# A four-layer graph network on one core: the second power of the adjacency by seven block products, and a last pair stored in two halves

## The chip, the core and the metric

The kernel runs on one core of a Trainium2 chip. A core has a matrix engine (TensorE, here PE, with a separate row PEld for its weight loads), three engines for elementwise work (VectorE or DVE, ScalarE or ACT, GpSimd or POOL) and an engine SyncE (SP) that here issues every DMA. Each engine executes its own queue in order; engines wait for each other through semaphores. The metric is the device time of one execution in microseconds (us). Times of the kernel before: 1476.92, 1478.15 and 1479.26 us, median 1478.15.

## The reference

The input is `x` of 64 graphs x 256 nodes x 128 features, with one 256 x 256 adjacency matrix `adj` (A below) for all of them. There are four layers, and each ends in a layer norm of `x + layer(x)`. All is in float32.

- Layer 0: five steps of a gated recurrent unit, each with a product of A and the state, then products with 128 x 128 weights, two sigmoids and a tanh.
- Layer 1: attention whose 256 x 256 matrix is made from A alone; products with it and with two weights.
- Layer 2: a graph attention with a softmax over 256 nodes per graph, then an isomorphism layer with another product with A, two weights and norms.
- Layer 3: a Chebyshev-like polynomial, in which both adjacencies are A:

```
parts = [x, A x, A^2 x, A^3 x, A x, A^2 x, A^3 x]
y     = sum_k parts[k] @ weight[:, :, k]
x     = layernorm(x + y)
```

The kernel forms q = A x and uses the second power of A: `x + y` is `x V0 + q V1 + A^2 (x V2 + q V3)`, with weights that are added up beforehand (the identity goes into V0). The last product, with A^2, is what the first part of the change is about.

## The kernel before

The 64 graphs are worked on in 32 pairs. One pair's features fill a tile of 128 partitions x 512 float32: two graphs, two blocks of 128 nodes each, 128 features. No loop over pairs orders the work. Instead the program records every operation of every pair as an `Op` in a `Schedule` (`S.add`, L120), with the values that it reads and writes, one or more ways to execute it (an engine, a planned cost in us and the function that issues it), and then a planner (`Schedule.order`, L161) simulates the engines with the planned costs and writes out one fixed order for each engine. At each step it takes the operation that can start first, and among equals the one whose due time `late` is earliest. Due times are set by pair (`due`, L139): 15 us apart, and `LAST_DUE` apart for the last twelve pairs. In every window of 15 us of the plan an entry of the table `SEEDS` (L63) can shift the due times by a fixed pseudo-random amount; another table of seeds gives another order. Operations with several ways, for example the sums that can go to DVE or POOL, go to the engine that the planner expects to finish first. `DVE+` marks a DVE operation for which the planner also books a port shared with POOL.

Intermediate values live in shared tiles (38 of the class A of 512 columns, eight PSUM banks of 512 columns, and others) that the planner assigns. Layouts are turned between token-major and feature-major in most places by DVE's 32 x 32 transpose and two DMA passes through DRAM (`turn`, L554 to L580).

Products of a pair with a 256 x 256 matrix are done in one of two ways:

- `spread` (L582) takes four matmuls of 256 columns (L588): for each graph, two blocks of the sum.
- `spread7` (L593) takes seven matmuls of 128 columns (L606), by Winograd's form of Strassen's scheme for 2 x 2 blocks. Sums of blocks of the right matrix are made once (`winograd`, L500). Per use it needs three sums of blocks of the state ahead of the products (L612 to L614), and copies and sums behind them (L620 to L627). Sums of SBUF operands alone are offered to DVE or POOL; copies out of PSUM (`evacuate`, L268) to ACT or DVE.

The table `SEVEN` (L24) says for how many of the last pairs the plain form is kept, by place.

Layer 3 (`layer3`, L888) turns x, forms q with `spread7`, and for pairs 0 to 29 calls `polynomial7` (L919). That computes the two products of [x q] with the weights again in seven block products (`product`, L937, whose matmuls are at L940), into the PSUM bank `y` (the part without A^2) and the tile `rr` (the part to be multiplied by A^2, written by DVE at L957 and L959). Then four matmuls of 256 columns (L963) add A^2 `rr` onto `y` in PSUM; `scale_norm` (L712) norms `y` and `store` (L884) writes the pair's 256 KB. A norm here needs no mean, since the weights are centred: it takes squares with an accumulated sum on ACT (L685), or statistics on DVE (L679); an added epsilon and a power of -0.5 on POOL (L690, L693); and a scaling on ACT (L705) or DVE (L707). The last two pairs, 30 and 31, go through the plain form in `layer3` (matmuls at L903, L904 and L911) with the same norm over the whole pair and one store.

Of the kernel before, what the change touches and what calls it, by code (L numbers as in the profile page):

```python
# [8 lines left out]
AF = mybir.ActivationFunctionType  # L9
# [11 lines left out]


FAST = (0, 1, 2, 3, 4)
SEVEN = {"q1": 4, "g": 4, "q3": 4, "pr": 2}  # L24
FIRST, FINAL = 1, 0
L1 = -1

# [22 lines left out]
SPARE = {"DVE": 1.0, "DVE+": 0.0, "POOL": -0.3}  # L50


DUE, LAST_DUE, LAST = 15.0, 12.0, 12

MARGIN, LAG = 1.1, 0.3

HOLD = (0.0, -20.0, 0.0, 40.0)

WINDOW, NUDGE = 15.0, 1.0

XLOAD, TLOAD = (0.6, 1.33, 2.5), (0.6, 1.05, 1.5)

SEEDS = [0, 113, 0, 0, 0, 0, 0, 0, 0, 0, 0, 0, 0, 0, 0, 0, 0, 0, 0, 0, 0, 0, 0, 0, 0, 0, 0, 0, 99747, 109039, 0,  # L63
         127395, 136626, 145860, 0, 172027, 0, 0, 192033, 202672, 213506, 0, 0, 0, 0, 0, 0, 0, 0, 0, 0, 0, 0, 0,
         0, 0, 0, 0, 0, 0, 0, 0, 0, 0, 431775, 441535, 451905, 0, 0, 0, 0, 0, 0, 516963, 526274, 0, 544854, 0, 0,
         0, 585026, 0, 0, 0, 622370, 631520, 639000, 646717, 658660, 667211, 0, 681297, 690347, 700377, 708021,
         726295, 727034, 736340, 0]


def mm(cols, n=1):  # L70
# [42 lines left out]
class Schedule:  # L113
# [47 lines left out]
    def order(self, tiles):  # L161

        self.prepare()
        engines = dict.fromkeys([*SEEN, "PORT"], 0.0)
        free = {cls: [(0.0, k) for k in range(len(ts))] for cls, ts in tiles.items()}
        ready, full, moved, out, window = [op for op in self.ops if not op.before], set(), 0.0, [], 0

        def slots(v):
            return [s for s in free[v.cls] if not v.seeded or (v.cls, s[1]) in full]

        while ready:
            best, homes, seed = None, {}, SEEDS[window] if window < len(SEEDS) else 0
            for op in ready:
                held = op.since
                for v in op.holds:
                    if v.home is None:
                        if (v.cls, v.seeded) not in homes:
                            homes[v.cls, v.seeded] = min((s for s, _ in slots(v)), default=1e9)
                        held = max(held, homes[v.cls, v.seeded])
                if held == 1e9 or best and held > best[0][0]:  # L180
                    continue
                way = None
                for engine, us, uses, spare, fn in op.plans:
                    start = max(held, *(engines[e] for e in uses))
                    if way is None or start + us + spare < way[0]:
                        way = start + us + spare, start, engine, us, uses, fn
                late = op.late
                if seed and op.pair >= 0:
                    late += NUDGE * (1 + seed % 3) * shuffled(op.number, seed)
                key = (way[1], late, op.number)  # L190
                if best is None or key < best[0]:
                    best = key, op, way
            if best is None:
                raise RuntimeError("the shared tiles are too few for this order")
            (start, _, _), op, (_, _, engine, us, uses, fn) = best
            if start >= (window + 1) * WINDOW:
                window += 1
                continue
            ready.remove(op)
            for v in op.holds:  # L200
                if v.home is None:
                    slot = min(slots(v), key=lambda s: s[0])
                    free[v.cls].remove(slot)
                    v.home, v.ap = slot[1], tiles[v.cls][slot[1]]
            end, base = start + us, engine.rstrip("+-")
            for e in uses:
                engines[e] = end
            seen = SEEN[base] + LAG
            if op.dma:
                wait, move, after = op.dma  # L210
                moved = max(moved, end + wait) + move * MARGIN
                seen = moved + after - end + LAG
            out.append((start, op.number, op, fn))
            for v in op.holds:
                v.left, v.end = v.left - 1, max(v.end, end + seen)
                if not v.left:
                    free[v.cls].append((v.end, v.home))
                    (full.add if v.full or v.seeded else full.discard)((v.cls, v.home))
            for x in op.then:
                same = engine != "SP" and x.base == base  # L220
                x.waits, x.since = x.waits - 1, max(x.since, end + (AGAIN.get(base, 0.0) if same else seen))
                if not x.waits:
                    ready.append(x)
        self.span = max(engines.values())
        return [(op, fn) for _, _, op, fn in sorted(out, key=lambda x: x[:2])]
# [11 lines left out]
def kernel(ctx: ExitStack, tc: tile.TileContext, x, xT, adj, adjT, mats, cols, rows, out):  # L237
# [54 lines left out]
        return rbc.ap[:, None, i * D:(i + 1) * D].to_broadcast([P, n, D])  # L292

    def load(o, i, v, kb=256, dma=None):
        S.add([("SP", 0.45, lambda: nc.sync.dma_start(o(), i))], [], [v], dma or (0.6, kb / 245, 0.9))

    xs = [Value("X", name=f"x{p}") for p in range(n_pairs)]
    hTs = [Value("T", name=f"hT{p}") for p in range(n_pairs)]
# [201 lines left out]
    def winograd(v, name):  # L500
# [5 lines left out]
                                                                             op0=ALU.mult, op1=ALU.subtract), [v, o], [o])  # L506
        dve(0.25, lambda: nc.vector.tensor_add(o.ap[:, 3, :], o.ap[:, 1, :], blk(1, 0)), [v, o], [o])
        return o
    aT7, offT7, ginT7 = winograd(aT, "aT7"), winograd(offT, "offT7"), winograd(ginT, "ginT7")
    centre(vx, lambda: vx.ap, 2)  # L510
    centre(vq, lambda: vq.ap, 2)
    vt = fixed([4, D], "vt")
# [30 lines left out]
    def tokens(v):  # L543
        return v.at(4, D)
# [9 lines left out]
    def turn(i, name, site, n=512):  # L554


        o = Value("A", name=name) if n == 512 else i
        if not by_dma(site):
            ts = [Value("PS", name="ps") for _ in range(n // 512)]
            for k, t in enumerate(ts):  # L560
                def fn(k=k, t=t):
                    for c in range(4):
                        nc.tensor.transpose(tokens(t)[:, c, :], i.at(n // P, P)[:, 4 * k + c, :], ident.ap)  # L563
                pe(TURN, fn, [i, ident], [t])
            for k, t in enumerate(ts):
                evacuate(lambda k=k: o.at(n)[:, 512 * k:512 * k + 512], lambda t=t: t.at(512), [t], [o])
            return o
        st, d = Value("A" if n == 512 else "B", name="turn"), Value("E", name="turn")
        dve(n / 512 * 0.55 + 0.09, lambda: nc.vector.transpose(st.at(n), i.at(n)), [i], [st])  # L569
        blocks = lambda *ap: bass.AP(tensor=d.ap.tensor, offset=d.ap.offset, ap=ap)  # L570
        S.add([("SP", 0.4, lambda: nc.sync.dma_start(blocks([P, P], [P * P, n // P], [1, P]), st.at(n // P, P)))],
              [st], [d], (0.6, n / 512 * 0.86, 0.5))

        def move():
            for q in range(4):
                b = blocks([P, 32], [32 * P, n // 32], [1, 32])
                nc.sync.dma_start(o.at(n // 32, 32)[32 * q:32 * q + 32],  # L577
                                  bass.AP(tensor=b.tensor, offset=b.offset + 32 * q, ap=b.ap))
        S.add([("SP", 2.1, move)], [d], [o], (-0.8, n / 512 * 1.5, 0.9))
        return o  # L580

    def spread(i, right):  # L582
# [229 lines left out]
    def layer2(x2):  # L812
# [14 lines left out]
        u, s = Value("B", name="u"), Value("S", name="nm")  # L827
        line = lambda *ap: bass.AP(tensor=d.ap.tensor, offset=d.ap.offset, ap=ap)
        dve(0.25, lambda: nc.vector.transpose(srow.at(4, 32), hs()[:, :, D - 30:D + 2]), [h], [srow])
        S.add([("SP", 0.45, lambda: nc.sync.dma_start(line([32, 4], [P, 4], [1, 32]), srow.at(4, 32)[31::32]))], [srow], [d], (0.5, 0.1, 0.5))  # L830
        S.add([("SP", 0.45, lambda: nc.sync.dma_start(sd.at(512), line([0, P], [1, 512])))], [d], [sd], (0.9, 0.7, 1.2))

        nm, den = (lambda k=k: s.at(32)[:, 4 * k:4 * k + 4] for k in range(2))
        d2v = Value("S", name="d2")
# [47 lines left out]
        layer_norm(y, x2)  # L882

    def store(o, p):  # L884
        S.add([("SP", 0.4, lambda: nc.sync.dma_start(out[2 * p:2 * p + 2].rearrange("b (t p) d -> p (b t) d", p=P), tokens(o)))],
              [o], [], (0.6, 1.0, 0.9))

    def layer3(x3, p):  # L888
# [19 lines left out]
        for i, t in enumerate(ts):  # L908
            def fn(i=i, t=t):
                for j in range(2):  # L910
                    nc.tensor.matmul(t.at(512)[:, :N], a2T.ap[:, j, i * P:(i + 1) * P], rr.at(2, N)[:, j],  # L911
                                     start=False, stop=(j == 1), skip_group_check=True)
            pe(mm(256, 2), fn, [a2T, rr, t], [t])
        s, rs = scale_stats([(t, range(i, 4, 2)) for i, t in enumerate(ts)])
        for i, t in enumerate(ts):
            scale_tokens(t, o, range(i, 4, 2), s, rs)
        store(o, p)

    def polynomial7(xT, qT, p):  # L919

# [36 lines left out]
        dve(0.335, lambda: nc.vector.tensor_add(R(1), blocks(t, 0), blocks(sv, 0)), [t, sv], [rr])  # L957
        product(t, 0, S4, VQ(1), [s4])
        dve(0.335, lambda: nc.vector.tensor_add(R(0), blocks(t, 0), blocks(sv, 1)), [t, sv], [rr])  # L959
        for i in range(2):  # L960
            def fn(i=i):
                for j in range(2):
                    nc.tensor.matmul(y.at(2, 2, D)[:, :, i, :], a2T.ap[:, j, i * P:(i + 1) * P], rr.at(2, 2, D)[:, j],  # L963
                                     start=False, stop=(j == 1), skip_group_check=True)
            pe(mm(256, 2), fn, [a2T, rr, y], [y])
        scale_norm(y, o)
        store(o, p)

    for p in range(n_pairs):
        S.pair = p  # L970
# [54 lines left out]
```

## Time and profile before

| | |
|---|---|
| median of three runs | 1478.15 us |
| the profiled execution | 1477.2 us |
| its span, first to last instruction | 1475.4 us |
| mean granted TensorE clock | 0.999 |
| PE busy | 1463.8 us, 99% |
| DVE busy | 1265.9 us, 86% |
| ACT busy | 1052.5 us, 71% |
| POOL busy | 931.5 us, 63% |
| mean DMA rate | 147 GB/s |
| L963, matmuls with A^2 | 240 instructions of 128x256, 59.6 us busy |
| L606, matmuls of `spread7` | 3346 instructions of 128x128, 275 ns each |
| L270, copy of 128x512 from PSUM on ACT | 592 ns |
| L621, sum of 128x256 | 464 ns on DVE, 751 ns on POOL |
| L625, sum of 128x128 | 321 ns on DVE, 512 ns on POOL |
| L693, power of 128x4 on POOL | 1073 ns |

The profile lists one execution, taken by the hardware profiler. Times are counted from the first instruction of the span. A line such as `L606 PE` names the line of the kernel that issued the instruction and the engine. The busy time of PE is a union over instructions that overlap; the pace at which matmuls follow each other is read from the chain of work, where each piece has the time that it adds. The chain follows the last instruction back to what released it, step by step. In the list of waits, "A <- B" means that A could have started but for B. A row by stretch gives the length, and then busy time and the number of instructions of each engine.

### The profile page before, as it was taken

The page shows a single profiled execution, that of the slowest core. Times are in us where ns is not written, and L with a number is a line of the kernel's source. Part 1 is how long each engine was busy: PE and PEld are TensorE (multiplying, and loading weights), DVE is VectorE, ACT ScalarE, POOL GpSimd, SP SyncE. Part 2 cuts the span into 40 slices and gives each one's busy share as a digit, 9 for nine tenths or more (in the row PEclk, how much of TensorE's full clock was granted, in tenths as well). Part 3 has the DMA queues.
Part 4 walks back from the last instruction along what each step waited for, and adds up shares of the span by engine and source line. Part 5 has one row for each costly group of instructions (what it writes and reads, how often), then busy time and mean ns, then how long its engine had stood idle before and what let it go on. Part 6 is the DMA issues. An engine that isn't in the chain of part 4 may idle for free.

```text
span 1475.4 us, 28934 instructions
## 1 busy us (share of the span) xinstructions
PE 1463.8 (99%) x8094; PEld 1065.6 (72%) x8094; DVE 1265.9 (86%) x3123; ACT 1052.5 (71%) x3246; POOL 931.5 (63%) x1440
## 2 busy tenths in 40 slices
PE   9999999999999999999999999999999999999998
PEld 6565666666677677777777777777767777788997
DVE  7867878898899999898888888888888898899883
ACT  4444565677778877876678677777777687879985
POOL 4523544457578778776667467566667576867753
PEclk9999999999999999999999999999999999999999
DMA  7635565777878998868878678786778778777662
GB/s 228 132 75 112 110 125 123 138 153 154 156 156 169 181 169 175 157 136 166 160 153 168 136 152 162 151 157 150 155 143 162 138 148 152 143 150 137 137 130 72
DMA packets 946847, 216.65 MB, mean 147 GB/s; under 512 B 726016, under 2 KB 942208, under 8 KB 946688
## 3 DMA queue, kind: packets, MB, share of 16 engines
q1 hardware_dynamic: 946688, 214.81, 72.1%
q8 instruction: 65, 1.06, 0.3%
q14 instruction: 94, 0.77, 0.2%
HBM read 116.86 MB, written 97.85 MB: 146 GB/s over the span
## 4 chain that ended last, share of the span: by engine, by line
PE 95%; DVE 2%; DMA 1%; ACT 1%; SPq 0%; issue 0%; POOLq 0%; ACTq 0%; POOL 0%; DVEq 0%
PE ps L606 24%; PE ps L732 9%; PE ps L739 9%; PE ps L740 9%; PE ps L724 9%; PE ps L725 9%; PE ps L761 7%; PE ps L940 6%; PE ps L861 4%; PE ps L963 4%; PE ps L588 2%; PE ps L821 2%; DMA a<-e 0%; SPq L577 0%; PE ps L563 0%
## 5 line engine op out<-in xcount | busy, mean ns | idle before, releaser
L606 PEld LDWEIGHTS ps<-aT,a 128*128 128x128 f32 x2208 | 301.9, 192 | 81.6 <-issue 73.5
L270 ACT COPY a<-ps 128x512 f32<-128x512 f32 (+2 forms) x590 | 246.1, 433 | 127.4 <-PE ps L606 58.1
L606 PE MATMUL ps<-aT,a 128*128 128x128 f32 x2208 | 330.6, 275 | 0.7 <-DVE a L612 0.5
L728 ACT ACTIVATE a<-ps,bzrh 128x512 f32<-128x512 f32 x160 | 110.1, 689 | 101.3 <-PE ps L725 95.0
L743 ACT ACTIVATE ps<-ps,bzrh 128x512 f32<-128x512 f32 x160 | 106.4, 665 | 94.5 <-PE ps L740 91.6
L685 ACT ACTIVATE a<-ps 128x128 f32<-128x128 f32 x508 | 134.2, 285 | 44.3 <-PE ps L761 19.4
L739 PE MATMUL ps<-a,w 128*128 128x512 f32 x320 | 163.6, 593 | 0.0
L740 PE MATMUL ps<-a,u5h 128*128 128x512 f32 x320 | 163.4, 592 | 0.0
L725 PE MATMUL ps<-a,w 128*128 128x512 f32 x320 | 163.4, 592 | 0.0
L627 DVE TENSOR_TENSOR a<-ps,a 128x256 f32<-128x256 f32 x239 | 99.5, 418 | 74.4 <-ACT a L270 37.6
L732 PE MATMUL ps<-a,w 128*128 128x512 f32 x320 | 162.7, 594 | 0.7 <-ACT a L728 0.6
L625 POOL TENSOR_TENSOR a<-a 128x128 f32<-128x128 f32 x204 | 103.5, 512 | 86.6 <-DVE a L621 71.7
L621 POOL TENSOR_TENSOR a<-a 128x256 f32<-128x256 f32 x125 | 93.5, 751 | 100.5 <-ACT a L270 95.8
L569 DVE STREAM_TRANSPOSE a<-a 128x512 f32<-128x512 f32 x215 | 149.3, 699 | 3.1 <-ACT a L705 0.8
L761 PE MATMUL ps<-W,a 128*128 128x128 f32 x1024 | 144.4, 275 | 0.0
L693 POOL TENSOR_TENSOR s<-s,neg_half 128x4 f32<-128x4 f32 x128 | 137.3, 1073 | 7.6
L761 PEld LDWEIGHTS ps<-W,a 128*128 128x128 f32 x1024 | 131.3, 192 | 12.6 <-issue 11.7
L734 ACT ACTIVATE a<-ps,bzrh 128x512 f32<-128x512 f32 x160 | 110.9, 694 | 35.3 <-PE ps L732 32.5
L724 PE MATMUL ps<-a,W 128*128 128x512 f32 x256 | 130.9, 593 | 0.0
L740 PEld LDWEIGHTS ps<-a,u5h 128*128 128x128 f32 x320 | 60.8, 190 | 76.5 <-issue 63.1
L725 PEld LDWEIGHTS ps<-a,w 128*128 128x128 f32 x320 | 60.8, 190 | 76.5 <-issue 63.8
L745 DVE SCALAR_TENSOR_TENSOR ps<-a,ps 128x512 f32<-128x512 f32 x160 | 109.4, 685 | 6.5 <-ACT a L734 5.2
(228 smaller groups left out, 3460.4 us busy)
## 6 DMA issues: line engine op xcount, KB each, us to landing
e<-a SPq DMA_DIRECT2D x277, 256.0 KB, 2.7
a<-e SPq DMA_DIRECT2D x1108, 64.0 KB, 2.2
e<-b SPq DMA_DIRECT2D x32, 512.0 KB, 3.3
b<-e SPq DMA_DIRECT2D x128, 128.0 KB, 3.9
x<-x_in SPq DMA_DIRECT2D x32, 256.0 KB, 4.4
t<-xT_in SPq DMA_DIRECT2D x32, 256.0 KB, 3.0
a<-d SPq DMA_DIRECT2D x32, 256.0 KB, 3.9
y_out<-a SPq DMA_DIRECT2D x32, 256.0 KB, 2.5
```

The source lines that it names most:

```text
L270: S.add([("ACT", us[0], lambda: nc.scalar.copy(o(), i())), ("DVE", us[1], lambda: nc.vector.tensor_copy(o(), i()))], r, w)
L569: dve(n / 512 * 0.55 + 0.09, lambda: nc.vector.transpose(st.at(n), i.at(n)), [i], [st])
L606: pe(mm(128), lambda: nc.tensor.matmul(blk(t, k), left(), rt(), start=start, stop=True, skip_group_check=True), [*r, right, terms, *[t] * ...
L685: nc.scalar.activation(tokens(junk)[:, c, :], v.at(len(tiles), D)[:, k, :], AF.Square, scale=D ** -0.5, accum_out=mv()[:, c, 1:2])
L693: pool(1.02, lambda: nc.gpsimd.tensor_tensor(rs(), rs(), neg_half.ap, op=ALU.pow), [s, neg_half], [s])
L724: nc.tensor.matmul(t.at(512), mat("u3"), hT.at(512), start=True, stop=False)
L725: nc.tensor.matmul(t.at(512), w4.ap, mT.at(512), start=False, stop=True)
L732: pe(mm(512), lambda t=t, mT=mT: nc.tensor.matmul(t.at(512), w3.ap, mT.at(512), start=False, stop=True, skip_group_check=True), [w3, mT, t ...
L734: act(0.59, lambda t=t, z=z: nc.scalar.activation(z.at(512), t.at(512), AF.Tanh, bias=bzrh.ap[:, 0:1], scale=0.5), [t, bzrh], [z])
L739: nc.tensor.matmul(t.at(512), w5.ap, mT.at(512), start=True, stop=False)
L740: nc.tensor.matmul(t.at(512), u5h.ap, r.at(512), start=False, stop=True)
L761: nc.tensor.matmul(tokens(t)[:, c, :], tokens(i)[:, c, :], w(), start=(first and k == c == 0), stop=(k == len(lefts) - 1), skip_group_chec ...
```

## The change

1. `polynomial7` hands the product with A^2 to a new function, `spread_on7`, for pairs 0 to 29. It does the four matmuls' work in seven block products of 128 columns: three sums of blocks of `rr` first, three products straight onto the bank `y`, four products into a second PSUM bank `t`. `t` is copied to SBUF (`evacuate`, ACT or DVE), its blocks are combined by three sums (DVE or POOL), and one DVE addition of 128x512 adds the result onto `y`. `winograd` is called once more, to make the sums of blocks of A^2.
2. The last pair (31) calls a new function, `finish`, for each of its two PSUM banks, that is for each half of the nodes. One graph's tokens are squared on ACT while the other's statistics are taken on DVE; POOL adds epsilon and takes the power for two columns; ACT scales one graph's tokens and DVE the other's; and each half is stored by a DMA of its own.
3. The planner's costs of DMA issues, `LAST_DUE` and `SEEDS` are changed. A further constant, `GROUP`, is 0.

```diff
-SEVEN = {"q1": 4, "g": 4, "q3": 4, "pr": 2}
+SEVEN = {"q1": 4, "g": 4, "q3": 4, "pr": 2, "a2": 2}
...
-DUE, LAST_DUE, LAST = 15.0, 12.0, 12
+DUE, LAST_DUE, LAST = 15.0, 10.0, 12
...
-SEEDS = [0, 113, 0, 0, 0, 0, 0, 0, 0, 0, 0, 0, 0, 0, 0, 0, 0, 0, 0, 0, 0, 0, 0, 0, 0, 0, 0, 0, 99747, 109039, 0,
+SEEDS = [0, 113, 389, 2033, 10562, 18537, 0, 26210, 32078, 38683, 45160, 51706, 59435, 64921, 73141, 0, 83634, 0,
...
-        S.add([("SP", 0.45, lambda: nc.sync.dma_start(o(), i))], [], [v], dma or (0.6, kb / 245, 0.9))
+        S.add([("SP", 0.52, lambda: nc.sync.dma_start(o(), i))], [], [v], dma or (0.6, kb / 245, 0.9))
...
-    aT7, offT7, ginT7 = winograd(aT, "aT7"), winograd(offT, "offT7"), winograd(ginT, "ginT7")
+    aT7, offT7, ginT7, a2T7 = (winograd(v, n) for v, n in ((aT, "aT7"), (offT, "offT7"), (ginT, "ginT7"), (a2T, "a2T7")))
...
-        S.add([("SP", 2.1, move)], [d], [o], (-0.8, n / 512 * 1.5, 0.9))
+        S.add([("SP", 2.1 if n == 512 else 2.7, move)], [d], [o], (-0.8, n / 512 * 1.5, 0.9))
...
+        if S.pair == n_pairs - 1:
+            for i, t in enumerate(ts):
+                finish(t, Value("A", name="last"), i, p)
+            return
...
+    def finish(t, o, i, p):
+
+        s, st, junk = Value("S", name="ms"), Value("S", name="st"), Value("A", name="junk")
+        v = lambda b: t.at(2, D)[:, b, :]
...
+        act(0.26, lambda: nc.scalar.activation(junk.at(D), v(0), AF.Square, scale=D ** -0.5, accum_out=mv(0)[:, 1:2]), [t], [m0, junk])
+
+        def by_dve():
+            nc.vector.bn_stats(st.at(6), v(1))
+            nc.vector.bn_aggr(mv(1), st.at(6))
+        dve(0.27, by_dve, [t], [m1, st])
+        pool(0.2, lambda: nc.gpsimd.tensor_scalar(rs(), var(), LN_EPS, None, op0=ALU.add), [m0, m1], [s])
+        pool(0.7, lambda: nc.gpsimd.tensor_tensor(rs(), rs(), neg_half.ap[:, :2], op=ALU.pow), [s, neg_half], [s])
+        act(0.26, lambda: nc.scalar.mul(half(0), v(0), rs()[:, 0:1]), [t, s], [r0])
+        dve(0.2, lambda: nc.vector.tensor_scalar(half(1), v(1), rs()[:, 1:2], None, op0=ALU.mult), [t, s], [r1])
+        S.add([("SP", 0.52, lambda: nc.sync.dma_start(out[2 * p:2 * p + 2, i * P:(i + 1) * P].rearrange("b p d -> p b d"), o.at(2, D)))],
+              [r0, r1], [], (0.6, 0.5, 0.9))
...
-        for i in range(2):
-            def fn(i=i):
-                for j in range(2):
-                    nc.tensor.matmul(y.at(2, 2, D)[:, :, i, :], a2T.ap[:, j, i * P:(i + 1) * P], rr.at(2, 2, D)[:, j],
-                                     start=False, stop=(j == 1), skip_group_check=True)
-            pe(mm(256, 2), fn, [a2T, rr, y], [y])
+        if S.pair < n_pairs - SEVEN["a2"]:
+            spread_on7(rr, y)
+        else:
...
+    def spread_on7(rr, y):
+
+        sv, m, t = Value("A", name="sums2"), Value("A", name="m2"), bank()
...
+        sum_(0.335, 0.69, lambda e: e.tensor_sub(sv.at(4, P)[:, 0:2], rr.at(4, P)[:, 0:2], rr.at(4, P)[:, 1::2]), [rr], [p1])
+        sum_(0.2, 0.42, lambda e: e.tensor_sub(s2(), s1(), H(0, 0)()), [rr, p1], [p2])
+        sum_(0.2, 0.42, lambda e: e.tensor_add(s4(), s2(), H(0, 1)()), [rr, p2], [p4])
+        product(t, 0, H(0, 0), B(0, 0), [rr], start=True)
+        product(t, 1, s1, T(0), [p1])
+        product(t, 3, s3, T(2), [p1])
+        product(t, 2, s2, T(1), [p2])
+        product(y, 0, H(0, 1), B(1, 0), [rr])
+        product(y, 2, H(1, 1), T(3), [rr])
+        product(y, 1, s4, B(1, 1), [p4])
+        evacuate(lambda: m.at(512), lambda: t.at(512), [t], [m])
+        sum_(0.335, 0.69, lambda e: e.tensor_add(sv.at(4, P)[:, 0:2], m.at(4, P)[:, 0:2], m.at(4, P)[:, 2:4]), [m], [p1])
+        sum_(0.335, 0.69, lambda e: e.tensor_add(m.at(4, P)[:, 1:3], m.at(4, P)[:, 1::2],
+                                                 blk(sv, 0)[:, None, :].to_broadcast([P, 2, P])), [p1, m], [m])
+        sum_(0.2, 0.42, lambda e: e.tensor_add(blk(m, 3), blk(sv, 0), blk(sv, 1)), [p1, m], [m])
+        dve(TT, lambda: nc.vector.tensor_add(y.at(512), y.at(512), m.at(512)), [y, m], [y])
```

In the changed kernel the matmul inside `product` of `spread_on7` stands at L1011, its first three sums at L1017 to L1019, those behind the copy at L1028, L1029 and L1031, and the last addition at L1032. Lines that were there before have moved down by 3 up to layer 3 and by more after it: L606 is L609, L270 is L273, L911 is L914, L940 is L968.

## The prediction

> **What bounds the kernel now.** I read the page's busy shares first, then the chain that ended last, then what TensorE (PE) waited for, then the busy time by stretch. The page:
>
> ```profile
> span 1475.4 us, 28934 instructions
> ...
> PE 1463.8 (99%) x8094; PEld 1065.6 (72%) x8094; DVE 1265.9 (86%) x3123; ACT 1052.5 (71%) x3246; POOL 931.5 (63%) x1440
> ...
> PE 95%; DVE 2%; DMA 1%; ACT 1%; SPq 0%; issue 0%; POOLq 0%; ACTq 0%; POOL 0%; DVEq 0%
> ```
>
> PE is busy for 99% of the span and carries 95% of the chain. The waits put down to PE (wait, then total, times, longest) hold nothing large:
>
> ```profile
> PE ps L330 <- DVE ones L328: 1.2, 1, 1.2
> PE ps L606 <- DVE a L880: 0.9, 1, 0.9
> PE ps L606 <- DVE a L612: 0.6, 2, 0.5
> ```
>
> The span minus PE's busy time is 11.6 us: 1.8 in the first 100 us, 6.7 after the last matmul, and about 3.2 scattered between. So nearly every microsecond of PE work taken out should shorten the run, provided the other engines keep up. Whether they do is a question of stretch (length, then busy time and count of PE, weight loads, DVE, ACT, POOL):
>
> ```profile
> 500.00:1300.00 800.00, 798.52 (x4539) 586.10 (x4538) 705.17 (x1759) 598.54 (x1881) 548.92 (x838) 1.00 0.78 155
> 1300.00:1425.00 125.00, 123.31 (x906) 112.45 (x905) 113.23 (x348) 110.73 (x436) 94.28 (x134) 1.00 0.70 141
> 1425.00:1476.00 51.00, 43.69 (x278) 39.89 (x276) 21.71 (x70) 33.43 (x137) 17.07 (x26) 0.97 0.32 72
> ```
>
> From 1300 to 1425 us DVE is idle for only 11.8 us, ACT for 14.3 and POOL for 30.7. The same count of L963's instructions gives 140 from 500 to 1300 us, 68 from 1300 to 1425 and 32 after: the step that is changed crowds into the stretch where the vector engines have least room.
>
> **The skill.** The Trainium skill's "Perfetto Trace Analysis", section "Identifying the Most-Contended Engine", warns that a matmul's busy time is a poor measure because pipelined instructions overlap. The trace agrees: a 128-column instruction shows 275 ns, but eight of them take 0.89 us in the chain, so I price PE from the chain. "SBUF — State Buffer", section "SBUF: two separate sides", says that a DVE instruction with two SBUF inputs and a GpSimd instruction reading SBUF take a shared port exclusively. The trace is in line with it: the 128x256 add that reads PSUM (L627) takes 418 ns, the same size from SBUF (L621) 464. "GPSIMD Engine Reference", section 3.1, has GpSimd 1.96 times slower in an add of 2048 elements; here it is 751 against 464 ns, 1.6 times. "PSUM — Partial Sum Buffer", "Specifications (TRN2)", bars GpSimd from PSUM, so the new copy out of PSUM and the final add fall to ACT and DVE; all PSUM readers in this trace are of these two.
>
> **Part 1, the second power on PE.** The chain in time shows both shapes (start, duration, instructions):
>
> ```profile
> 1325.81 1.73 PE ps L963 x8
> ...
> 1337.24 0.89 PE ps L940 x8
> ```
>
> Each f32 matmul stands as two instructions in the trace (the order has 120 of L963, the trace 240). A 256-column matmul costs 2 x 1.73/8 = 0.433 us, a 128-column one 2 x 0.89/8 = 0.223. The order of the changed kernel has none of the 120 left and 210 new ones of 128x128. Per pair: 4 x 0.433 = 1.73 goes, 7 x 0.223 = 1.56 comes, 0.166 saved. Thirty pairs (0 to 29): **-5.0 us**. Every other PE count is equal.
>
> **Part 2, the vector work bought with it.** Per pair one PSUM copy of 128x512 (592 ns on ACT), one DVE add of 128x512 into PSUM (685, by L745), and six sums. By the order, of the 180 sums 52 of 128x256 and 20 of 128x128 are on DVE, 38 and 70 on POOL. On DVE, with 0.44 and 0.31 us: 22.9 + 6.2 + 30 x 0.685 = 49.7 us. On POOL, with 0.77 and 0.51: 29.3 + 35.7 = 65 us. ACT: 30 x 0.592 = 17.8. The planner moves other work off DVE: 17 sums of L612 (0.46), 14 of L657 (0.376), 5 of L852 (0.795), 9 of L871 (0.755), 6 of L870 (0.43) go, against 7 more of L867 and L868 (0.74), together some -21; what leaves DVE lands on POOL and, with 14 of L662 and 20 of L804, on ACT. With a few smaller ones the net is about **+25 us DVE, +85 us POOL, +30 us ACT**. That brings DVE to 1291 of about 1470 (88%), POOL to 1017 (69%), ACT to 1083 (74%). Over the run all fit under PE, where it costs nothing. In 1300 to 1425 it is tight: 68/8 = 8.5 pairs' share is 0.28 of the net, +7 on DVE against 11.8 idle, +24 on POOL against 30.7, +8 on ACT against 14.3. It fits only if nothing comes late: without that cover each microsecond too much is a microsecond of PE. The new copy to PSUM, three sums and the last add have no PE instruction behind them, only the norm and the store, so they delay PE only by occupying engines, one more PSUM bank of eight, and y's bank for longer. The three sums ahead of the products are on PE's path, between L959 and the first products, and are covered by other pairs' matmuls.
>
> Bounds for the added PE waiting: -3 (the new order also loses the 3.2 us scattered now) to +9 (8.5 pairs x (1.65 DVE + 0.6 ACT) = 19 us, less the 11.8 of DVE idle, plus 2 for other stretches). I take **+1.5**: DVE would stand at 120 of 124 us there, and a queue that full makes some operands late.
>
> **Part 3, the last pair.** The tail now (start, duration):
>
> ```profile
> 1467.16 1.58 PE ps L911 x6
> ...
> 1468.93 0.46 ACT a L685 x3
> 1469.39 0.08 issue
> 1469.47 0.22 POOL s L690
> 1469.70 0.04 issue
> 1469.74 1.08 POOLq L1021
> 1470.81 0.02 issue
> 1470.84 0.37 ACT a L705
> 1471.20 0.26 ACTq L1021
> 1471.46 0.52 ACT a L705 x2
> ```
>
> PE ends at 1468.73, the scaling at 1471.98, the span at 1475.4, with the 256 KB store between. After: the two last tokens' squares were 0.66 us after PE's end; one square on ACT (0.28 with its 0.2 read, overlapped: 0.37) beside a bn_stats and aggregate on DVE (0.275 + 0.15, overlapped: 0.34) ends at 0.42: -0.24. The power is taken of two columns, a size the trace does not show; between 0.52 (proportional) and 1.04 (fixed) I take 0.75: -0.3, and 0.15 back, since the first half's power occupies POOL until the second's statistics are ready. Scaling: one 128x128 each on ACT and DVE, 0.3 instead of 1.14: -0.8. The store of 128 KB: the 256 KB one moves in about 1.05 us (at 290 GB/s), so -0.45; its bound is 0 if latency is all. The first half's store issue (0.37 on SP) lies under the second half's power. Sum **-1.6** (bounds -0.6 to -2.1).
>
> **Part 4, what only moves.** Planner costs of SP issues (0.45 or 0.4 to 0.52), LAST_DUE 12 to 10 and other seeds change no instruction but reorder all queues, DMA issues included: SP keeps 1714 entries plus one store. The last pairs come nearer together. I put its effect into the bounds of part 2. The four DVE instructions that form a2T7 (about 2 us, in the first 100 us, DVE busy 73%) are wanted only near 520 us: 0.
>
> Sum: 1475.4 - 5.0 - 1.6 + 1.5 = 1470.3 us of span. The profiled execution took 1477.2 and the median is 1478.15, 2.75 above the span: **1473.1 us**.
>
> **Rivals.** *B, the gain is used up:* from 1300 us DVE and the port become the bound and PE waits 4 to 9 us more. For it speaks DVE's 90.6% there before anything is added; against it, that PE kept 98.6% in that very stretch. Middle: 1478.15 - 6.6 + 6 = 1477.5, no measurable change. *C, the order also improves:* late waits go and PE's scattered idle time falls by 2 to 3 us: 1478.15 - 6.6 - 2 = 1469.5. For it: nothing but order causes those waits; against it, fuller queues. *D, slower:* the shared port serialises DVE and POOL from 1300 us: 8.5 x (1.65 + 2.15) = 32 us of new port time against 11.8 us of DVE idle; 20 us of PE waiting at worst, 1491 us. It decides once waiting exceeds 6.6 + 3 = 9.6 us. Against it: from 500 to 1300 us POOL ran 69% beside DVE's 88% with PE at 99.8%. That the change does nothing is excluded by the order's counts.
>
> **How the numbers follow.** No change can be told within 0.2%, 1475.2 to 1481.1 us. Forecast (waiting 0 to 3.5): 0.55, 1471.6 to 1475.1. C 0.17, below. B 0.20, 1475.6 to 1480.5. D 0.08. Faster 0.70 (forecast and C, less a little), same 0.21, slower 0.09. Leaving out 1 in 10 at each end, D and a little of B above and the end of C below: 1469.2 to 1478.8.
>
> **What would show it.** Right: PE's busy time near 1459, eight-fold 1.73 us pieces of the square gone from the chain and 0.22 ones in place, PE's end to span's end about 5.1 us, PE waits after 1300 us of at most 5 us. Wrong: PE waiting on the new sums (L1017 to L1019) or on copies by ACT after 1300 us with DVE above 96%, which is B or D; the power on two columns still at 1.04; or new waits in the stretches before 1300 us, which would mean that the reordering, not the crowding, sets the result.

## The result and the profile after

The changed kernel takes 1476.38 us (median of 20 runs, 1475.18 to 1478.23) against 1478.13 for the kernel before on the same chip: ratio 0.9987, 95% interval 0.9981 to 0.9994. That is a gain of 0.13%: the interval excludes no change at all, but the gain is inside the 0.2% that the prediction called no measurable change. The time lies in the stated range only because the range also held rival B; the forecast itself, 1473.1, was missed by 3.3 us.

The page of the changed kernel, the same lines as before:

```profile
span 1474.2 us, 29700 instructions
...
PE 1462.0 (99%) x8274; PEld 1068.6 (72%) x8274; DVE 1293.2 (88%) x3185; ACT 1078.7 (73%) x3315; POOL 1010.0 (69%) x1574
...
PE 93%; DVE 3%; POOL 2%; ACT 1%; DMA 1%; issue 1%; SPq 0%; POOLq 0%; ACTq 0%; DVEq 0%
```

The vector engines took on what was forecast: DVE 27 us more, POOL 79, ACT 26. PE's busy time fell by 1.8 us only, although its work fell by more. The chain shows the new price (start, duration, instructions): the 14 instructions of seven products take 1.56 us. The plain form, which is left for the last two pairs only (L914), takes 1.73:

```profile
1458.64 1.56 PE ps L1011 x14
...
1461.06 1.73 PE ps L914 x8
```

Busy time hides short waits, since matmuls overlap and a started matmul is drawn to its modelled end. So I add up something else from the trace's records. Following matmuls start 112 ns apart with 128 columns, 216 with 256 and 430 with 512; PE's **work** is the number of instructions times these, and its **waits** are what lies between two starts above that, where it is over 30 ns. In us, from one profile each:

| | work | waits, 0-20 us | 20-400 | 400-600 | 600-1300 | from 1300 | all waits | PE's end to span's end | span |
|---|---|---|---|---|---|---|---|---|---|
| before | 1461.7 | 3.2 | 0.1 | 1.1 | 1.8 | 2.9 | 9.1 | 6.70 | 1475.4 |
| changed | 1456.9 | 3.5 | 0.8 | 3.4 | 0.3 | 5.6 | 13.5 | 5.95 | 1474.2 |
| changed, again | 1456.9 | 3.0 | 0.8 | 2.5 | 0.1 | 5.6 | 12.0 | 5.95 | 1472.7 |

PE's work fell by 4.8 us, the end by 0.75, and the waits rose by 4.4 (2.9 in the second profile). The paces are rounded up, so work, waits and end add to some 2 us more than the span in every row; it is the differences between rows that count. The two profiles of the changed kernel differ by 1.5 us of waits, so I judge gains by timed runs and use the waits for where they are. The list of PE's waits in the changed kernel has no large item (total, times, longest):

```profile
PE ps L591 <- DVE a L750: 1.2, 1, 1.2
PE ps L333 <- DVE ones L331: 1.2, 1, 1.2
PE ps L727 <- ACT a L273: 0.9, 1, 0.9
PE ps L591 <- ACT a L273: 0.5, 1, 0.5
PE ps L609 <- ACT x L708: 0.5, 1, 0.5
PE ps L968 <- DVE a L985: 0.5, 1, 0.5
PE ps L609 <- POOL a L615: 0.4, 1, 0.4
PE ps L864 <- DMA b<-e: 0.4, 1, 0.4
```

None of them is a wait for the new sums L1017 to L1019. But the first, which lies at 1350 us, stands behind new work in DVE's queue: the last addition of a pair (L1032) is executed just before the operation that PE waits for (L750).

```profile
1350.05 0.69 DVE L1032 TENSOR_TENSOR ps<-ps,a 128x512 f32<-128x512 f32 x1
...
1350.65 0.68 DVE L750 SCALAR_TENSOR_TENSOR a<-ps,a 128x512 f32<-128x512 f32 x1
```

By stretch (length, then PE, weight loads, DVE, ACT, POOL):

```profile
500.00:1300.00 800.00, 799.13 (x4668) 590.60 (x4667) 718.81 (x1795) 617.80 (x1938) 602.46 (x926) 1.00 0.78 156
1300.00:1425.00 125.00, 122.38 (x947) 112.24 (x946) 120.61 (x348) 114.17 (x435) 107.05 (x155) 1.00 0.66 136
1425.00:1476.00 51.00, 43.24 (x309) 40.33 (x307) 31.18 (x98) 36.29 (x145) 28.18 (x46) 0.95 0.30 73
```

From 1300 to 1425 us DVE is now busy 120.6 of 125 (96.5%), as the prediction's sum had it.

The last pair's end is the second surprise. The timeline of the changed kernel (start, duration, engine, what; in brackets the idle time and what ended it):

```profile
1467.98 0.30 DVE L937 BATCH_NORM_STATS2 s<-ps 128x6 f32<-128x128 f32 x1 [5.58 <-ACT a L934]
1468.30 0.28 ACT L934 ACTIVATE a<-ps 128x128 f32<-128x128 f32 x1 [0.35 <-PE ps L914]
...
1468.70 0.30 DVE L937 BATCH_NORM_STATS2 s<-ps 128x6 f32<-128x128 f32 x1 [0.20 <-ACT a L934]
1468.97 0.71 POOL L941 TENSOR_TENSOR s<-s,neg_half 128x2 f32<-128x2 f32 x1
...
1470.73 0.37 ACT L942 ACTIVATE a<-ps,s 128x128 f32<-128x128 f32 x1 [0.64 <-POOL s L941]
1471.13 0.35 DVE L943 TENSOR_SCALAR a<-ps,s 128x128 f32<-128x128 f32 x1 [0.66 <-ACT a L942]
```

DVE never reads a bank beside ACT: its statistics start when ACT's square of that half has ended, its scaling when ACT's has ended. In the trace both DVE instructions wait for a semaphore that ACT updates, although the statistics use nothing that the square writes. The scaling ends at 1471.48, 3.2 us after PE's end (1468.28), as before (3.25); only the smaller store is gained.

### The profile page after: what moved, and what is told of

Same layout as the page of the kernel before. It is cut to its first block, busy times and chain, and to the rows that moved or that the text cites. A ratio compares the mean times of both kernels' runs of the same rounds, so it can differ in the third digit from the quotient of the medians.

```text
span 1474.2 us, 29700 instructions
## 1 busy us (share of the span) xinstructions
PE 1462.0 (99%) x8274; PEld 1068.6 (72%) x8274; DVE 1293.2 (88%) x3185; ACT 1078.7 (73%) x3315; POOL 1010.0 (69%) x1574
## 4 chain that ended last, share of the span: by engine, by line
PE 93%; DVE 3%; POOL 2%; ACT 1%; DMA 1%; issue 1%; SPq 0%; POOLq 0%; ACTq 0%; DVEq 0%
PE ps L609 24%; PE ps L735 9%; PE ps L742 9%; PE ps L743 9%; PE ps L727 9%; PE ps L728 9%; PE ps L764 7%; PE ps L968 6%; PE ps L864 3%; PE ps L1011 3%; PE ps L591 2%; PE ps L824 2%; POOL s L696 1%; DVE b L839 0%; POOL s L651 0%
## 5 line engine op out<-in xcount | busy, mean ns | idle before, releaser
L609 PEld LDWEIGHTS ps<-aT,a 128*128 128x128 f32 x2208 | 297.3, 192 | 78.2 <-issue 69.1
L273 ACT COPY a<-ps 128x128 f32<-128x128 f32 (+2 forms) x618 | 259.5, 442 | 105.2 <-PE ps L609 49.2
L609 PE MATMUL ps<-aT,a 128*128 128x128 f32 x2208 | 324.3, 275 | 0.5 <-ACT x L708 0.5
L728 PE MATMUL ps<-a,w 128*128 128x512 f32 x320 | 163.4, 592 | 0.0
L696 POOL TENSOR_TENSOR s<-s,neg_half 128x4 f32<-128x4 f32 x127 | 142.4, 1122 | 6.8
L624 POOL TENSOR_TENSOR a<-a 128x256 f32<-128x256 f32 x123 | 92.0, 750 | 72.9 <-ACT a L273 72.1
L615 POOL TENSOR_TENSOR a<-a 128x256 f32<-128x256 f32 x97 | 72.3, 746 | 64.8 <-DMA a<-e 44.2
L728 PEld LDWEIGHTS ps<-a,w 128*128 128x128 f32 x320 | 60.8, 190 | 76.5 <-issue 65.3
```

Source lines behind the costliest of these rows:

```text
L273: S.add([("ACT", us[0], lambda: nc.scalar.copy(o(), i())), ("DVE", us[1], lambda: nc.vector.tensor_copy(o(), i()))], r, w)
L609: pe(mm(128), lambda: nc.tensor.matmul(blk(t, k), left(), rt(), start=start, stop=True, skip_group_check=True), [*r, right, terms, *[t] * ...
L696: pool(1.02, lambda: nc.gpsimd.tensor_tensor(rs(), rs(), neg_half.ap, op=ALU.pow), [s, neg_half], [s])
L728: nc.tensor.matmul(t.at(512), w4.ap, mT.at(512), start=False, stop=True)
```

## The experiments

Each kernel was timed against the kernel before on its own chip, and differences of medians are against that. In the runs "in its own order" the planner plans every operation as in the kernel named, and only what is issued differs, so that all other instructions keep their places.

**1. The vector work taken out of the changed kernel.** Five trailing operations per pair are planned but not issued, and then the three leading sums as well:

```diff
+        first = len(S.ops)
         evacuate(lambda: m.at(512), lambda: t.at(512), [t], [m])
...
         dve(TT, lambda: nc.vector.tensor_add(y.at(512), y.at(512), m.at(512)), [y, m], [y])
+        for op in S.ops[first:]:
+            op.skip = True
```

> The changed kernel in its own order, but the five vector operations behind the second power's products (the copy out of PSUM, three sums and the last addition, of pairs 0 to 29) are planned and not issued; their contribution is missing from the output. Crowding (the new vector work makes PE wait): PE's idle time above its pace, 13.5 us in the changed kernel, falls by 3 us or more, most of it from 1300 us on; time about 1473. Reordering (the new order itself holds the waits): the waits stay, those between 480 and 540 us above all; time 1475.5 or more.

> As the run before, and the three sums ahead of the products are not issued either (the products read blocks of rr itself, so the output is not the second power). Only the seven matmuls per pair are left of the new work, in the changed kernel's order. Crowding: about 1472.5, with the wait after 1300 us below 1.5 us. Reordering: 1475 or more, and the waits between 480 and 540 us stay.

Measured: 1474.65, 3.0 us below before, ratio 0.9984 (0.9977 to 0.9991); and 1474.11, 3.6 below, 0.9977 (0.9969 to 0.9984). The changed kernel itself has 0.9987 and, again, 0.9985. By ratios, dropping the five operations gives 0.2 to 0.4 us, which can't be told from nothing, and dropping all eight 1.2 to 1.5 us, with intervals that still overlap a little. The waits from 1300 us on fall from 5.6 to 3.8 and 3.6 (2.9 before the change); those from 400 to 600 us stay in the second run (3.0). So crowding is seen after 1300 us and is worth about 1 us. It is not where most of the gain went.

The wait at 1350 us shows how such a wait comes and goes. Without L1032 in the queue it is gone in the first run. In the second it is back (1.0 us), because another DVE operation ahead of it, which takes 0.69 us in the changed kernel, took 1.76 beside one on POOL:

```profile
1347.57 1.48 POOL L875 TENSOR_TENSOR a<-a,rbc 128x512 f32<-128x512 f32 x1
1347.84 1.76 DVE L812 TENSOR_TENSOR a<-x,rbc 128x512 f32<-128x512 f32 x1
```

**2. PE's saving alone, in the order of the kernel before.** Seven matmuls, four and then three, stand where the four stood. The vector work of the seven products is left out, so what they add is not A^2 `rr`.

```diff
             def fn(i=i):
-                for j in range(2):
-                    nc.tensor.matmul(y.at(2, 2, D)[:, :, i, :], a2T.ap[:, j, i * P:(i + 1) * P], rr.at(2, 2, D)[:, j],
-                                     start=False, stop=(j == 1), skip_group_check=True)
+                for k in range(4 - i):
+                    nc.tensor.matmul(y.at(512)[:, k * P:(k + 1) * P], a2T.ap[:, k % 2, i * P:(i + 1) * P],
+                                     rr.at(512)[:, k * P:(k + 1) * P], start=False, stop=True, skip_group_check=True)
```

> The kernel before in its own order; only the four matmuls of 256 columns are replaced where they stand by seven of 128 columns on blocks of rr, with no vector work added (the output is not the second power). PE's step alone: 30 x 0.166 = 5.0 us less, 1473.1. If time taken out of PE comes back as waits on the other engines because these are just as late: 1475 to 1477.

Measured: 1476.61, 1.1 us below before, ratio 0.9994 (0.9986 to 1.0002). The work is 1456.9, 4.8 us less, and the waits are 14.3 instead of 9.1. They sit all over the run: 4.8 us of them from 600 to 1300, where there were 1.8, and 4.3 from 1300, where there were 2.9. PE's list now has these (of the kernel before, L612 stood at 0.6 and L728 at 0.6):

```profile
PE ps L606 <- DVE a L612: 1.6, 3, 0.7
...
PE ps L732 <- ACT a L728: 0.9, 1, 0.9
PE ps L861 <- issue: 0.9, 1, 0.9
PE ps L606 <- DVE a L880: 0.9, 1, 0.9
PE ps L725 <- ACT a L270: 0.6, 1, 0.6
PE ps L861 <- DMA b<-e: 0.5, 1, 0.5
PE ps L940 <- DVE a L957: 0.5, 1, 0.5
```

This is the run that decides. Without any new vector work and without any new order, most of the time taken from PE comes back as waits: even the favourable end of the interval leaves a gain of 2.1 us of the 4.8. PE reaches operands of DVE, ACT and the transfers before they are there. At 99% busy PE looked like the only bound, and the others were only just in time.

**3. Is it DVE's load?** One DVE operation of 0.69 us is left out in each of the 160 steps of layer 0, in the kernel before, in the run of experiment 2, and in the changed kernel, each in its own order.

```diff
             dve(TT, lambda t=t, hT=hT: nc.vector.tensor_sub(t.at(512), t.at(512), hT.at(512)), [t, hT], [t])
+            S.ops[-1].skip = True
```

> The kernel before in its own order, without one DVE operation of each step of layer 0 (the subtraction of the state from the candidate, in place in PSUM; 160 times 0.69 us, so about 100 us less of DVE; the output is not the reference's). PE is the bound and DVE only causes its scattered waits: 2 to 4 us less than before, 1474. DVE is no part of it: no change.

> The same with the four matmuls of the second power replaced in place by seven, as in the earlier run without vector work, which gave 1 us instead of 5. If time taken from PE came back as waits on a DVE that is just as late, the whole 5.0 us now show against the run with the relief alone: about 1469. If the other engines, the transfers or the latency of the chains hold PE, the difference stays at 1 to 2 us: 1472 to 1473.

> The changed kernel in its own order with the same relief. DVE held the gain back: 5.5 us below the kernel before with the relief (4.8 of PE, 0.75 of the end), about 1468.5. Else: 2 us below it, as without relief.

Measured, with before at 1477.05: 1475.85 (ratio 0.9992, 0.9985 to 0.9998); 1473.39 (0.9966, 0.9954 to 0.9978); 1475.15 (0.9982, 0.9976 to 0.9988). In the order of before, the seven matmuls gain 2.5 us by medians (3.8 by the ratios) with DVE relieved, against 1.1 (0.9) without. That hints that DVE's load holds back a part of the gain, but it is not shown: the relieved run has five executions, the intervals of the two gains overlap (about 1.8 to 5.8 and -0.3 to 2.1), and in the profiles the waits rise by 5.2 us with relief (5.5 to 10.7) just as without (9.1 to 14.3).

In the changed kernel's order the relief of some 87 us of DVE (1205.7 busy instead of 1292.3) gains next to nothing: 0.9982 against 0.9985 to 0.9987. But layer 0 is mostly over by 1300 us. Of the 87 us only 2.4 fall from 1300 to 1425 (118.2 us busy instead of 120.6), so this run says little of the stretch where DVE is fullest. Before it, where nearly all of the relief falls, the waits stay: 3.1 us from 400 to 600. From 1300 they are 4.2. The list:

```profile
PE ps L610 <- ACT a L274: 0.8, 1, 0.8
PE ps L592 <- DVE a L752: 0.6, 1, 0.6
PE ps L592 <- ACT a L274: 0.5, 1, 0.5
PE ps L610 <- ACT x L709: 0.5, 1, 0.5
PE ps L610 <- DVE a L616: 0.4, 1, 0.4
```

L592 is the changed kernel's L591 here, L610 its L609, so much the same places wait. The wait at 1350 us is halved, from 1.2 to 0.6. DVE's total load over the run is not what sets the waits before 1300 us; what stands in its queue just ahead of an operand can.

**4. The order.** The changed kernel's constants with the plain second power for all pairs, and the reverse: its code with the seeds, due times and DMA costs of the kernel before. Here the planner makes a new order for each.

```diff
-SEVEN = {"q1": 4, "g": 4, "q3": 4, "pr": 2, "a2": 2}
+SEVEN = {"q1": 4, "g": 4, "q3": 4, "pr": 2, "a2": 32}
```

> The changed kernel with the plain second power for all pairs: only the planner's new costs, due times and seeds and the last pair's halves are left, and the planner makes an order of its own for it. PE's work is 4.8 us more than in the changed kernel. If the gain went into crowding by the new vector work, the waits are as in the kernel before (9 us above PE's pace): 1476.9. If the new plan is itself worse, they stay near 13 us: 1481.

> The changed kernel's code with the planner's constants of the kernel before (its seeds, 12 us between the last due times, its costs of DMA issues): the new operations alone, ordered by a plan that was not chosen for them. If the gain went into the new vector work whatever the order: about as the changed kernel, 1475 to 1477, with waits of some 12 to 13 us above PE's pace. If what the waits are depends on the order chosen, as the run with the new plan alone suggests (17.7 us of waits): 1479 to 1484, waits of 16 us or more, and the change without its seeds would be a loss.

Measured: 1484.67, ratio 1.0052 (1.0039 to 1.0064), 7.2 us slower than before; and 1500.43 against 1478.21, ratio 1.0147 (1.0123 to 1.0171), 22 us slower. Both are beyond what either theory expected. The first has the PE work of the kernel before and 17.7 us of waits instead of 9.1. The second has the same PE instructions as the changed kernel, by number and size, and 40.0 us of waits instead of 13.5; 31.4 of them are after 1300 us. Its stretches and the head of its list:

```profile
1300.00:1425.00 125.00, 114.84 (x848) 103.15 (x847) 116.45 (x349) 103.01 (x382) 103.81 (x154) 0.97 0.64 127
1425.00:1502.00 77.00, 60.90 (x405) 54.63 (x403) 46.96 (x150) 50.16 (x192) 34.56 (x53) 0.93 0.40 87
```

```profile
PE ps L904 <- DMA a<-e: 3.6, 1, 3.6
PE ps L607 <- ACT a L271: 3.5, 5, 1.2
PE ps L589 <- DVE a L985: 2.9, 1, 2.9
PE ps L862 <- DMA b<-e: 1.8, 1, 1.8
```

From 1300 to 1425 us DVE is less busy than in the changed kernel (116.5 against 120.6), while PE waits for single chains of the last pairs, up to 3.6 us for a transfer. Not all of the 40.0 us is waiting. In two stretches of 6.8 us, from 1382.5 and from 1484.9, the granted clock is 0.5, and two instructions of 256 columns take 0.85 us there; in the changed kernel they take 0.43:

```profile
1488.47 0.85 PE ps L904 x2
```

```profile
1462.79 0.43 PE ps L906 x2
```

This makes up 5.5 of the 40.0 us. The two stretches begin within PE's two longest waits (L589 and L904 in the list). In the first run one stretch of 3.4 us makes up 1.6 of the 17.7.

So the waits depend on which operation stands where, and in both crossings constants and operations that were not used together lose. The new operations under the old constants are a loss of 22 us; with the new constants the change comes out just ahead. Seeds, due times and DMA costs were exchanged together, so how much each is worth is not shown.

**5. The last pair.** The old tail put back in the changed kernel's order; then each half on ACT alone; then the first half on ACT and the second on DVE.

```diff
-        act(0.26, lambda: nc.scalar.activation(junk.at(D), v(0), AF.Square, scale=D ** -0.5, accum_out=mv(0)[:, 1:2]), [t], [m0, junk])
+        on_act = i == 0
+        act(0.26, squares if on_act else nothing, [t], [m0, junk])
-        dve(0.27, by_dve, [t], [m1, st])
+        dve(0.27, nothing if on_act else by_dve, [t], [m1, st])
```

Here `squares` and `by_dve` do both graphs' tokens of the half; the scalings are divided alike.

> The changed kernel in its own order with the last pair normed as before: all four squares and all four scalings on ACT, one power of four columns, one store of 256 KB. The prediction's step 3 (the halves are worth 1.6 us): 1478.0. What the trace of the changed kernel suggests (ACT and DVE take turns, the gain is 0.75 us): 1477.1.

> The changed kernel once more, to be compared on one chip with the variants of its last pair: as before it, a ratio of about 0.9987 to the kernel before, and a wait of some 13 us above PE's pace.

> The changed kernel in its own order; each half of the last pair is squared and scaled on ACT alone, DVE's part of it is gone. If the split over ACT and DVE runs in parallel, as step 3 of the prediction has it, this makes each half's statistics 0.1 and its scaling 0.3 us longer: slower by 0.4 us. If DVE waits for ACT on the same PSUM bank, as the trace of the changed kernel reads: the second half's statistics end 0.4 us sooner, its scaling 0.1 sooner; PE's end to the span's end 5.95 to about 5.4 us.

> The changed kernel in its own order; the last pair's first half is normed on ACT alone, the second on DVE alone, so each engine has a PSUM bank of its own. Turns on one bank: DVE no longer waits for ACT, PE's end to the span's end 5.95 to about 5.3 us. Parallel split: about as now or longer.

Measured: the old tail 1476.85 with before at 1477.68, ratio 0.9993 (0.9985 to 1.0001), and from PE's end to the span's end 6.56 us instead of 5.95. So without the halves, the new square in the new order gains 0.8 us, which can't be told from nothing. The other three, with before at 1477.46: the changed kernel 1475.18, 0.9985 (0.9977 to 0.9993); on ACT alone 1474.33, 0.9977 (0.9971 to 0.9984), end 5.58; one engine for each half 1474.43, 0.998 (0.9974 to 0.9987), end 5.44. In the last one DVE's statistics follow PE:

```profile
1467.44 0.50 DVE L941 BATCH_NORM_STATS2 s<-ps 128x6 f32<-128x128 f32 x2 [5.97 <-PE ps L914]
```

Giving one engine a half is quicker than splitting it over two, by 0.4 to 0.5 us in the profiles. The medians agree (0.75 to 0.85 lower), but the intervals overlap. Both variants are faster than the kernel before, by 0.2%, and have the lowest medians of the complete kernels here. The Trainium skill's "PSUM — Partial Sum Buffer", section "PSUM bank collisions raise a hardware error", has a reason that fits: two engines on one bank (and one quarter of its partitions) at once raise an error, reads by ACT and DVE included, and the compiler's scheduler adds a dependency between them. The traces agree on the dependency: DVE's statistics start after ACT when both read one bank and right after PE when DVE has the bank to itself. That the collision itself would occur was not tried.

## Why the prediction was right or wrong

- **What bounds the kernel: wrong.** "Nearly every microsecond of PE work taken out should shorten the run" is the step that failed. Experiment 2 took 4.8 us out and got 1.1. That PE never waited long was read as slack on the other side; it was balance. The condition attached to the step ("provided the other engines keep up") was tested by sums of busy time per stretch, which can't see it: in experiment 2 DVE was idle for over 12% of the time from 600 to 1300 us, and 3 us of new waits still appeared there. By the sum, the span came out 3.9 us longer than expected: 2.9 of it waits, 0.85 the halves, 0.2 the price. That the time lies in the range is owed to the room that was left for rival B, and not to this step.
- **Its own signs.** The prediction named new waits before 1300 us as a sign that the reordering, and not the crowding, sets the result. That sign came: from 400 to 600 us the waits rose from 1.1 to 3.4 and 2.5. The other sign came in part: DVE was above 96% from 1300 to 1425 us and the waits from 1300 us passed 5 us (5.6), but none of those listed was for the new sums themselves.
- **Part 1, the price: right** as work: 4.8 us for 5.0.
- **Part 2, the vector work: right in amount** (DVE +27 for +25, POOL +79 for +85, ACT +26 for +30; DVE at 120.6 of 125 where 120 was expected). **The waiting of +1.5 was mis-sized:** +4.4 and +2.9 in two profiles. Taking all vector work out returned 1.2 to 1.5 us by ratios, so as the price of crowding the term was about right, as far as the noise allows to say. The rest, waits that come with less PE work and another order, was not in the sum at all.
- **Part 3, the halves: wrong size and mechanism.** -1.6 was expected, -0.75 measured (-0.6 against the old tail in the same order). The statistics on DVE "beside" the square on ACT, -0.24, and the scaling "on ACT and DVE, 0.3 instead of 1.14" assumed that both engines read one bank together. They take turns: DVE's statistics and scaling each wait for ACT's. The power of two columns, 0.71 us for an estimated 0.75, was right.
- **Part 4, the order: wrong.** It was costed only as part of the bounds of the waiting. With the same PE instructions, orders differ by 24 us (1476.4 and 1500.4), of which 5.5 are the lower clock in the profile of the second. It is the largest effect that any run here shows.
- **Rivals.** B came true in size: 1477.5 expected, 1476.4 measured. Its mechanism, DVE and the port as the bound from 1300 us, is only partly so: waits there rose by 2.7 us and fell by about 2 when the vector work was left out, but waits rose before 1300 us too, and experiment 2 lost most of the gain without any new vector work. D did not happen with the new seeds. Its size, 1491, was passed with the old ones, where PE's longest waits were for single chains and transfers.
- **The port.** The prediction read it from means, 418 ns for an add that reads PSUM against 464 from SBUF. The median of the second (L621 on DVE) is 419: most take the same time, and a few take up to 1482. L812 in experiment 1 is such a long one: it took 1.07 us longer than the same operation in the changed kernel, beside one on POOL. That fits two engines that exclude each other, but no run separates it.

Open: which of DVE's queue, ACT, the transfers and the latency of single chains holds how much of the remaining gain. DVE's load was tried, but hardly after 1300 us; ACT's and the transfers' were not. Experiment 3's runs also shorten layer 0's chain by one operation, so what they gain is not load alone.

## What to carry to other kernels

In this kernel, whose order is fixed ahead and packed to 99% of one engine, a saving on that engine was worth little by itself, because the other engines were only just in time. In another such kernel, take the saving without its side work in the old order first: that run prices it. Then look at the order: here the same PE instructions took 24 us more or less by it. And before splitting work over two engines, look whether both read the same PSUM bank; if they do, give each engine banks of its own.

## What was not expected of the hardware

POOL's power has a large fixed part. It takes 713 ns with two columns and 1037 with four (the median; the mean of 1073 in the kernel before holds some longer ones). An estimate from these two: about 0.32 us for two columns on each partition, and 0.39 whatever the size.

The granted clock fell to 0.5 within the run in the two orders with the most waits, for 6.8 us twice and for 3.4 us once. In the kernel before and in the changed kernel it stayed at 1.00 until after PE's last matmul. What length of pause brings the lower clock isn't shown here: in the order with old constants it began within waits of 2.9 and 3.6 us and not within one of 1.8, and in the other order it came after two waits of about 1 us, one soon after the other.
